# Nine groups' second MLP matmul as seven block products beside a convolution, with one weight loaded late

## The chip, the cores and the metric

The kernel runs on one core of one Trainium2 chip. The metric is device time in microseconds (us), the median of several executions. In the profile PE is TensorE's matmul, PEld its weight load, DVE is VectorE, ACT ScalarE, POOL GpSimd, SP the engine that issues most transfers; every float32 matmul leaves two PE records.

## The reference

Two blocks act on x of shape (2, 56, 56, 384), 6272 tokens of 384 channels, in float32. The first is neighbourhood attention (12 heads, 7 by 7 windows) with an MLP. The second projects to 768 channels, convolves each channel 3 by 3, smooths the result along rows and columns both ways, normalizes, projects back and ends with another MLP. Cut to what matters:

```python
# block 0
x = x + neighborhood_attention(layer_norm(x), w_qkv, rpb, w_proj)
y = layer_norm(x)
x = x + gelu(y @ w1 + b1) @ w2 + b2            # 384 -> 1536 -> 384
# block 1
p = layer_norm(x) @ w_in + b_in                # 384 -> 768
local = depthwise_conv_3x3(p, k_conv)
mixed = 0.25 * (ema_left + ema_right + ema_down + ema_up)(local) + local
x = x + layer_norm(mixed) @ w_out + b_out      # 768 -> 384
x = x + gelu(layer_norm(x) @ w1 + b1) @ w2 + b2
```

## The kernel before, in words

The attention comes first and is not touched. After it `passes` does the rest in two passes over the tokens. The first pass takes the MLP of block 0 and the projection `w_in` of block 1; the second takes `w_out` and the MLP of block 1.

**Groups.** The 49 tiles of 128 tokens are cut into `groups`: group 0 has one tile, groups 1 to 12 have four. In each group the first matmul of the MLP (`hidden`, L1206, on `columns`, L1195) goes through twelve blocks m of 128 hidden channels, three matmuls of 128x512 each. Then `project_in` runs the *previous* group's six blocks of `w_in`, whose input has been normalized meanwhile (`ahead_of`), and stores them to `p_d` in DRAM. Then the second matmul of the MLP follows.

**Two forms of the second matmul.** `tokens` (L1213) is the plain one: for each of four tiles twelve matmuls of 128x384 (`y` and `y_end` are two PSUM banks used in turn, `bank`). ScalarE has copied the residual into the bank ahead (`seeded`, L1223), and copies the result out (L1889). `tokens_by_seven` (L1669) treats the group's tokens and the hidden and output channels as 2x2 blocks and computes the product from seven block products rather than eight, 84 matmuls of 128x192. It needs sums of the hidden blocks (`sums_of_hidden`, L1644 to L1646, and `last_sum`, L1677, on GpSimd), sums of the weight blocks made once (`sums_of_w2`, L1638), and puts the products together with ScalarE copies and VectorE and GpSimd adds (L1683 to L1715). Groups 1 and 2 (`EARLY`) use the second form, as do nine groups at the end of the second pass; group 3 (`EARLY.stop`) has its first matmul by seven products and its second by `tokens`; groups 4 to 12 are plain throughout.

**The convolution beside.** From group 3 on a queue of jobs, `Beside`, is worked off on VectorE between TensorE's instructions. A `Band` is some rows of one 128-channel block of one image: eight multiply-adds (L1302) for the taps, after a first one on ScalarE (L1285) or VectorE (L1287), then a scan forth and back along the rows (L1248, L1252). A `Columns` job takes the whole plane the other way: it turns it with copies (L1348), scans it forth and back twice and adds the result to what is stored. ScalarE scales a band's result (L1317), and GpSimd issues the accumulating transfer to `mix_d` (L1321). The order on each engine is the program's, so `Beside.go` decides by bookkeeping how much of the queue stands between two steps of TensorE:

```python
def go(self, worth, own=0.0):
    self.due += self.rate * worth - own
    while self.due > 0.0:
        step = self.step()
        if step is None: self.due = 0.0
        else: self.due -= step
```

`worth` is TensorE's step (`MLP` 2.6 for a hidden block, `ROW` 7.8 for a tile of `tokens`), `rate` is 1.06, `own` what VectorE has to do besides (`STATS` 0.75 for one tile's statistics), and each step gives an estimate of its own time. Loading a job that was not loaded ahead books 8.0. `beside.later` issues transfers and scalings some steps after the work that they need. `beside.until` works the queue off up to a job; it stands before the last group, for image 0, and in the second pass before the tail, for image 1.

**Buffers.** The pool `io` has two buffers each of `mx` (a group's 768 projected channels), `xc` (a group's result x2) and hT. `w_out` is loaded at the start, and `prepare_w_out` folds the normalization into it in group 4: six narrow matmuls (L1146), a transfer of the column sums to DRAM and back (`sums_d`), and seven VectorE operations. In groups 4 to 12 the transposed inputs go through three `pt` banks (`to_channels`, L269 on TensorE and L272 on ScalarE).

Of the kernel before, what the change touches and what calls it, by code (L numbers as in the profile page):

```python
# [42 lines left out]
P = 128  # L43
# [133 lines left out]
def block_kernel(ctx: ExitStack, tc: tile.TileContext, ins: dict, out: bass.AP):  # L177
# [914 lines left out]
    def passes(xs, xn, w1, w2, between=lambda ps: None):  # L1092
# [5 lines left out]
        cctx, bctx, fctx = ExitStack(), ExitStack(), ExitStack()  # L1098
# [15 lines left out]
        w_out = wp.tile([P, NI, C], F32, name="w_out")  # L1114
# [12 lines left out]
        turns, hids = [], []  # L1127
# [11 lines left out]
        def prepare_w_out():  # L1139
# [4 lines left out]
            for c in range(NI):  # L1144
                yield
                nc.tensor.matmul(  # L1146
                    ps[:2, :], lhsT=pair[:, c, :], rhs=w_out[:, c, :],
                    start=c == 0, stop=c == NI - 1,
                )
# [8 lines left out]
            for _ in range(3):  # L1158
# [10 lines left out]
        def channels(xn, n, g, b):  # L1169
            hT = io.tile([P, NC, MT], F32, name="hT")  # L1170
            to_channels(ps_t, [xn[:, k, :] for k in range(n)], hT, NC, g, b, tag)
# [245 lines left out]
        def load_mix(g):  # L1417
            t0, n = dgroups[g]
            mx = io.tile([P, NI, MT], F32, name="mx")
# [37 lines left out]
        def measure_beside(m, g, ahead):  # L1457
# [3 lines left out]
            k = m // 2 - 1  # L1461
            if m == 4:
                add_row(ahead[1], n, "b_out")
            if m == 10:
# [6 lines left out]
        def project_out(g, mx, x, inner, then=lambda k: None):  # L1471
            n = dgroups[g][1]
            x3 = io.tile([P, NT, C], F32, name="xc")
# [15 lines left out]
        for w, name in ((w_in, "L1_conv_w_in"), (w_out, "L1_conv_w_out")):  # L1489
            nc.sync.dma_start(out=w, in_=ins[name].rearrange("(c p) n -> p c n", p=P))  # L1490
        load_row(1, "b_out")
# [6 lines left out]
        waiting = xn_w = hT_w = xn_next = cp = decay = None  # L1498
# [3 lines left out]
        def project_in(g, hT, between=lambda: None, at=1):  # L1502
            t0, n = groups[g]
            pt = io.tile([P, NI, MT], F32, name="mx")
# [125 lines left out]
        def sums_of_w2(w2, engine=nc.gpsimd):  # L1630
# [4 lines left out]
            t1, t2, t3, t4 = (tp.tile([P, q, C // 2], F32, name=f"w2_t{i}") for i in range(4))  # L1635
# [12 lines left out]
        def tokens_by_seven(low, high, s1, s2, w2, w2_sums, src, dst):  # L1648
# [10 lines left out]
            u1, u2 = (tp.tile([P, 2, hc], F32, name=x) for x in ("u1", "u2"))  # L1659
# [21 lines left out]
            def result(engine, half, c, t):  # L1681
                at = slice(2 * half, 2 * half + 2), slice(c * hc, (c + 1) * hc)
                engine.tensor_tensor(dst[:, at[0], at[1]], t, src[:, at[0], at[1]], ALU.add)  # L1683
# [13 lines left out]
            product(bank_z, 1, summed(s1), t1)  # L1697
            for p in range(2):
# [3 lines left out]
            nc.vector.tensor_tensor(u2, bank_z, u2, ALU.add)  # L1702
            product(bank_a, 1, of(high, 0), b21)
            last_sum(1)
            result(nc.gpsimd, 1, 1, u2)
            result(nc.vector, 0, 0, bank_a)
            yield
            for p in range(2):
# [3 lines left out]
            yield  # L1712
            for p in range(2):
                product(bank_z, p, of(high, 0), b22)
            nc.vector.tensor_tensor(u1, bank_z, u1, ALU.add)  # L1715
# [393 lines left out]
```

## Time and profile before

| what | value |
|---|---|
| median of 3 runs | 2569.69 us (2568.74 to 2572.11) |
| the profiled execution | 2573.64 us, of which the span of its instructions is 2571.8 |
| PE busy | 2545.4 us, 99% of the span |
| DVE busy | 1973.7 us, 77% |
| ACT busy | 1115.9 us, 43% |
| POOL busy | 560.9 us, 22% |
| granted TensorE clock | 0.996 |

A busy share is a mean over very different stages; the stage of the first pass lies between 670 and 1640 us, the convolution between 890 and 1910. Lines of groups read: source line, engine, operation, result<-inputs, shapes, count, busy time, mean duration. Lines of the timeline read: start, duration, engine, line, operation, and in brackets how long the engine had been idle and what ended that. A window's line has busy time and count for PE, PEld, DVE, ACT and POOL, then the granted clock, the share of DMA time and GB/s.

### The profile page before, as it was taken

The page shows a single profiled execution, that of the slowest core. Times are in us where ns is not written, and L with a number is a line of the kernel's source. Part 1 is how long each engine was busy: PE and PEld are TensorE (multiplying, and loading weights), DVE is VectorE, ACT ScalarE, POOL GpSimd, SP SyncE. Part 2 cuts the span into 40 slices and gives each one's busy share as a digit, 9 for nine tenths or more (in the row PEclk, how much of TensorE's full clock was granted, in tenths as well). Part 3 has the DMA queues.
Part 4 walks back from the last instruction along what each step waited for, and adds up shares of the span by engine and source line. Part 5 has one row for each costly group of instructions (what it writes and reads, how often), then busy time and mean ns, then how long its engine had stood idle before and what let it go on. Part 6 is the DMA issues. An engine that isn't in the chain of part 4 may idle for free. (4 is left out here: it accounts for less than half of the span.)

```text
span 2571.8 us, 41605 instructions
## 1 busy us (share of the span) xinstructions
PE 2545.4 (99%) x16438; PEld 1695.7 (66%) x16438; DVE 1973.7 (77%) x3785; ACT 1115.9 (43%) x2030; POOL 560.9 (22%) x610
## 2 busy tenths in 40 slices
PE   9999999999999999999999999999999999999999
PEld 5666666666688645554455555555568888888888
DVE  3888878887544299967999958988887877878861
ACT  4656555555333444344454443333762233233222
POOL 0111111111443011101110011011123333333332
PEclk9999999999999999999999999999999999999999
DMA  6432454225511256655675655777781333333210
GB/s 210 161 100 87 151 190 153 88 85 191 158 43 38 79 147 173 167 132 149 178 273 191 183 174 162 239 208 191 187 213 24 74 74 74 74 74 74 47 28 21
DMA packets 162159, 338.50 MB, mean 132 GB/s; under 512 B 12086, under 2 KB 113952, under 8 KB 159648
## 3 DMA queue, kind: packets, MB, share of 16 engines
q1 hardware_dynamic: 128064, 251.18, 29.1%
q0 software_dynamic: 28944, 57.81, 13.7%
q10 hardware_dynamic: 4944, 26.74, 3.1%
q8 instruction: 131, 2.15, 0.3%
q14 instruction: 76, 0.62, 0.1%
HBM read 171.91 MB, written 134.88 MB: 119 GB/s over the span
## 5 line engine op out<-in xcount | busy, mean ns | idle before, releaser
L1302 DVE SCALAR_TENSOR_TENSOR loc<-pt,taps,loc 128x495 f32<-128x495 f32 (+13 forms) x432 | 397.8, 921 | 25.2 <-ACT loc L1285 9.4
L1195 PE MATMUL mm<-hT,w 128*128 128x512 f32 x864 | 378.6, 593 | 0.6 <-ACT hT L272 0.6
L1195 PEld LDWEIGHTS mm<-hT,w 128*128 128x128 f32 x864 | 161.6, 190 | 193.8 <-issue 185.2
L571 ACT ACTIVATE pts<-pts 119x448 f32<-119x448 f32 (+5 forms) x396 | 210.8, 573 | 110.4 <-DVE pts L561 101.5
L561 DVE TENSOR_TENSOR pts<-sc,bias 119x448 f32<-119x448 f32 (+5 forms) x396 | 219.0, 615 | 45.7 <-PE sc L550 45.4
L1213 PE MATMUL y<-w,hid 128*128 128x384 f32 x648 | 213.6, 486 | 0.2 <-ACT y L1223 0.2
L1213 PE MATMUL y_end<-w,hid 128*128 128x384 f32 x648 | 213.4, 486 | 0.0
L404 PE MATMUL ps<-hT,wqkv 128*128 128x448 f32 x504 | 207.7, 557 | 2.1 <-ACT vs L449 1.5
L1448 DVE STREAM_TRANSPOSE turned<-mx 32x192 f32<-32x192 f32 x528 | 194.8, 369 | 6.9
L1178 DVE STREAM_TRANSPOSE hT<-xn 32x96 f32<-32x96 f32 x656 | 176.8, 270 | 26.0 <-ACT xn L255 17.6
L1206 ACT ACTIVATE hid<-mm,chan 128x512 f32<-128x512 f32 x144 | 98.5, 686 | 185.4 <-PE mm L1195 185.4
L1213 PEld LDWEIGHTS y_end<-w,hid 128*128 128x128 f32 x648 | 122.7, 190 | 84.5
L1213 PEld LDWEIGHTS y<-w,hid 128*128 128x128 f32 x648 | 122.3, 190 | 84.3 <-ACT y L1223 0.8
L1195 PE MATMUL mm<-hT,w_in 128*128 128x512 f32 x396 | 171.9, 593 | 0.6 <-DVE hid_u L1599 0.6
L404 PEld LDWEIGHTS ps<-hT,wqkv 128*128 128x128 f32 x504 | 92.5, 192 | 86.1 <-issue 76.0
L1195 PEld LDWEIGHTS mm<-hT,w_in 128*128 128x128 f32 x396 | 75.1, 190 | 94.9 <-issue 88.8
L1321 POOL DMA_DIRECT2D mix_d<-both x54 | 52.2, 966 | 350.6 <-ACT both L1317 213.4
L227 POOL TENSOR_TENSOR rs<-rs,mhalf 128x4 f32<-128x4 f32 (+4 forms) x56 | 53.8, 960 | 331.1 <-DVE rs L224 321.2
L550 PEld LDWEIGHTS sc<-qT,kT 32*100 32x100 f32 (+3 forms) x3168 | 87.8, 169 | 46.4 <-DVE sum L580 7.6
L590 PE MATMUL o<-pts,vt 100*32 100x112 f32 (+3 forms) x3168 | 116.6, 264 | 0.8 <-ACT pts L571 0.8
L620 PE MATMUL ps<-wproj,og 128*128 128x384 f32 x294 | 107.0, 504 | 2.8 <-DVE og L533 2.1
L550 PE MATMUL sc<-qT,kT 32*100 32x112 f32 (+3 forms) x3168 | 106.5, 268 | 3.1 <-DVE pts L561 3.1
(197 smaller groups left out, 4649.5 us busy)
## 6 DMA issues: line engine op xcount, KB each, us to landing
loc<-loc_d SPq DMA_DIRECT2D x24, 784.0 KB
xa<-x_d SPq DMA_DIRECT2D x24, 768.0 KB
xa<-rows POOLq DMA_DIRECT2D x24, 768.0 KB, 8.6
bias<-in_bias_t ACTq DMA_DIRECT2D x13, 1344.0 KB
p_d<-mx SPq DMA_DIRECT2D x11, 1536.0 KB
mx<-mix_d SPq DMA_DIRECT2D x11, 1536.0 KB
v_d<-vs SPq DMA_DIRECT2D x49, 192.0 KB
xr<-in_x SPq DMA_DIRECT2D x49, 192.0 KB
```

The lines of the kernel that those rows point to most:

```text
L404: nc.tensor.matmul(ps, lhsT=wqkv[:, c, m * P : (m + 1) * P], rhs=hT[:, c, half_of(n)], start=c == 0, stop=c == NC - 1,)
L550: nc.tensor.matmul(sc[i // 2][: w.keys, i % 2, q : q + TT], lhsT=kT[d, hg, w.keys_at + r * w.kc : w.keys_at + (r + w.rows) * w.kc], rhs=qT ...
L561: nc.vector.tensor_tensor(self.pts[:n, h : h + 2, lo:hi, :], sc[half][:n, :, at * TT : (at + hi - lo) * TT].rearrange("p h (c q) -> p h c ...
L571: nc.scalar.activation(t, t, AF.Exp)
L590: nc.tensor.matmul(o[i * HD : (i + 1) * HD, self.slot, :TT], lhsT=w.vt[:n, c, h * HD : (h + 1) * HD], rhs=self.pts[:n, i, c, :], start=c = ...
L620: nc.tensor.matmul(ps, lhsT=ogs[t // 7][:, c, at : at + P], rhs=wproj[:, c, :], start=c == 0, stop=c == NC - 1,)
L1178: nc.vector.transpose(hT[j : j + HD, :, k * P + i : k * P + i + HD], xn[i : i + HD, k, :].rearrange("p (c q) -> p c q", c=NC)[:, :, j : j ...
L1195: nc.tensor.matmul(ps[:, : n * P], lhsT=w[:, c, m * P : (m + 1) * P], rhs=hT[:, c, : n * P], start=c == 0, stop=c == NC - 1,)
L1206: nc.scalar.activation(t[:, : n * P], ps[:, : n * P], AF.Gelu, bias=col(b1, m))
L1213: nc.tensor.matmul(ps, lhsT=t[:, k * P : (k + 1) * P], rhs=w[:, m, :], start=m == 0 and onto is None, stop=m == len(lhs) - 1, skip_group_c ...
L1302: nc.vector.scalar_tensor_tensor(to, pt[:, lo + dy - self.top : hi + dy - self.top, xt : xt + n], self.tap(dy, dx), to, ALU.mult, ALU.add,)
L1448: nc.vector.transpose(t[j : j + HD].rearrange("p (m c) -> p m c", m=NI)[:, :, i : i + HD], mx[i : i + HD, :, k * P + j : k * P + j + HD],)
```

## The change

Groups 3 to 11, nine of them, take `tokens_by_seven` in place of `tokens`. In groups 4 to 11 the first matmul stays plain, and `sums_of_hidden` follows each pair of its blocks that belong together, at m = 7, 9 and 11. The last group, 12, keeps `tokens`.

The sums of the weights and of the hidden blocks get a pool of their own, `dp`, that lives until the last group. Room for it is made in two ways: `mx` and `xc` have one buffer until then, and `w_out` is no longer loaded at the start. At the last group `dp` is closed, a pool `late` takes its place with the second buffers and `w_out`, and `prepare_w_out` moves there, with two matmuls at each step in place of one.

Inside `tokens_by_seven` the products change order (b22 before t4), the bank `y_end` is copied out by ScalarE (`uz`) so that one of the adds moves from VectorE to GpSimd, and the intermediate results lie in x2's own memory where that is free. The products need one more PSUM bank (`wide_b`), so `pt` has two buffers, and the transposes of groups 4 to 11 use `y`, `y_end` and one `pt` bank. Cut to its core:

```diff
+        w_out = late = None
+        def wide(name, shape):
+            second[name] = late is not None and not second[name]
+            return late.tile(...) if second[name] else io.tile(shape, F32, name=name, bufs=1)
...
         def prepare_w_out():
             ps = bank()
             for c in range(NI):
-                yield
+                if c % 2 == 0:
+                    yield
...
-            for _ in range(3):
+            for _ in range(2):
                 yield
...
         def channels(xn, n, g, b):
-            to_channels(ps_t, [xn[:, k, :] for k in range(n)], hT, NC, g, b, tag)
+            to_channels(
+                ps_t, [xn[:, k, :] for k in range(n)], hT, NC, g, b, tag,
+                banks=[t() for t in turning] if turning else None,
+            )
...
         def measure_beside(m, g, ahead):
-            k = m // 2 - 1
-            if m == 4:
+            k = m // 2 - (2 if g == 0 else 1)
+            if m == 4 and g:
                 add_row(ahead[1], n, "b_out")
-            if m == 10:
+            if m == 10 and g:
                 ahead[2].close(n)
...
         def tokens_by_seven(low, high, s1, s2, w2, w2_sums, src, dst):
+            if src is dst:
+                u1, u2, uz = (tp.tile([P, 2, hc], F32, name=x) for x in ("u1", "u2", "u3"))
+            else:
+                u1, u2, uz = part(dst, 0, 1), part(dst, 1, 1), part(dst, 1, 0)
...
             product(bank_z, 1, summed(s1), t1)
+            nc.scalar.copy(uz, bank_z)
+            product(bank_a, 1, of(high, 0), b21)
+            last_sum(1)
+            yield
+            result(nc.vector, 0, 0, bank_a)
             for p in range(2):
                 product(bank_b, p, of(low, 1), t3)
             nc.scalar.copy(u2, bank_b)
             yield
-            nc.vector.tensor_tensor(u2, bank_z, u2, ALU.add)
-            product(bank_a, 1, of(high, 0), b21)
-            last_sum(1)
+            nc.gpsimd.tensor_tensor(u2, uz, u2, ALU.add)
             result(nc.gpsimd, 1, 1, u2)
-            result(nc.vector, 0, 0, bank_a)
+            for p in range(2):
+                product(bank_z, p, of(high, 0), b22)
             yield
+            nc.vector.tensor_tensor(u1, bank_z, u1, ALU.add)
+            result(nc.gpsimd, 0, 1, u1)
             for p in range(2):
                 product(bank_b, p, of(high, 1), t4)
             yield
             result(nc.vector, 1, 0, bank_b)
-            yield
-            for p in range(2):
-                product(bank_z, p, of(high, 0), b22)
-            nc.vector.tensor_tensor(u1, bank_z, u1, ALU.add)
-            result(nc.gpsimd if src is dst else nc.vector, 0, 1, u1)
...
+            seven = early or half_early or 0 < g < last
             if g == last:
                 beside.until((0, NI - 1))
+                dctx.close()
+                late = pctx.enter_context(tc.tile_pool(name="late", ...))
                 ahead = load_mix(0)
+                w_out = late.tile([P, NI, C], F32, name="w_out")
+                load_weights(w_out, "L1_conv_w_out")
+                preparing = prepare_w_out()
                 beside.rate = 0.98
+                for t in (y_end_wide, ps_y.tile([P, MT], F32, name="turn", tag="y")):
+                    primed(t)
...
                     hid.append(hidden(w1, m, hT, n, "L0_conv_b1"))
+                    if seven and m % 2 == 1 and m > NHID // 2:
+                        u = (m - NHID // 2) // 2
+                        sums_of_hidden(u, hids[-4], hids[-1], s1, s2)
...
+            elif seven:
+                for i, _ in enumerate(tokens_by_seven(low, high, s1, s2, w2, w2_sums, x, x2)):
+                    beside.go(ROW / 2, 2 * STATS + 0.5 if i == 6 else 0.5 if i in (3, 5) else 0.0)
+                    if i == 6:
+                        for k in range(2):
+                            norm.add(k, [x2[:, k, :]])
...
-            for k in range(n) if g >= EARLY.stop else ():
+            for k in range(n) if g == last else ():
                 ps = tokens(hid, w2, k, onto=seeds.pop(0))
```

## The prediction

> **What bounds the kernel now.** I read the busy line first, then the stretch of the nine changed groups, then who waits there, then the two forms of the matmul in order of time. The page:
>
> ```profile
> PE 2545.4 (99%) x16438; PEld 1695.7 (66%) x16438; DVE 1973.7 (77%) x3785; ACT 1115.9 (43%) x2030; POOL 560.9 (22%) x610
> ```
>
> TensorE is the bound. Groups 4 to 11 and then the stretch to the tail, by window (columns: PE, PEld, DVE, ACT, POOL busy):
>
> ```profile
> 912.31:1557.40 645.09, 645.09 (x1838) 330.30 (x1837) 555.18 (x636) 276.39 (x429) 85.30 (x76) 1.00 0.62 176
> 1557.40:1920.20 362.80, 360.26 (x1109) 195.40 (x1108) 317.37 (x359) 174.99 (x261) 61.14 (x54) 1.00 0.74 198
> ```
>
> PE never pauses in these eight groups (645.09 of 645.09), but VectorE, which runs the convolution beside it, has only 89.9 us to spare, 11.2 a group. Nearly all of it is one wait, for the next band's rows when the job queue has run dry:
>
> ```profile
> DVE loc L1287 <- DMA pt<-p_d: 87.4, 5, 26.1
> ```
>
> **What the change buys on PE.** One group in the old form, in order of time, then an early group that has the new form already:
>
> ```profile
> 1046.83 7.91 PE L1213 MATMUL y<-w,hid 128*128 128x384 f32 x24
> ...
> 1070.05 7.90 PE L1213 MATMUL y_end<-w,hid 128*128 128x384 f32 x24
> 1077.79 7.46 PE L1195 MATMUL mm<-hT,w 128*128 128x512 f32 x17
> ```
>
> ```profile
> 805.25 4.06 PE L1669 MATMUL y<-w,hid 128*128 128x192 f32 x24
> ...
> 828.65 4.06 PE L1669 MATMUL y_end<-w,hid 128*128 128x192 f32 x24
> 832.55 1.03 PE L1580 MATMUL ua<-hT,w 128*128 128x256 f32 x4
> ```
>
> Old: 1077.79 - 1046.83 = 30.96 us for 96 records of 128x384. New: 832.55 - 805.25 = 27.30 us for 168 records of 128x192. Saved 3.66 us a group, times 9: **-32.9 us**.
>
> [...] where the two meet, at the tail's weight sums:
>
> ```profile
> 1911.95 1.35 DVE L1638 TENSOR_TENSOR w_t<-w 128x1152 f32<-128x1152 f32 x1
> 1913.34 2.02 DVE L1638 TENSOR_TENSOR w_t<-w,w_t 128x1152 f32<-128x1152 f32 x1
> 1915.28 1.87 DVE L1638 TENSOR_TENSOR w_t<-w 128x1152 f32<-128x1152 f32 x1
> 1917.07 1.88 DVE L1638 TENSOR_TENSOR w_t<-w,w_t 128x1152 f32<-128x1152 f32 x1
> ```
>
> ```profile
> 1912.82 1.31 POOL L1561 TENSOR_TENSOR xsums<-hT 128x256 f32<-128x256 f32 x1
> 1914.21 1.73 POOL L1561 TENSOR_TENSOR xsums<-xsums,hT 128x256 f32<-128x256 f32 x1
> 1915.90 1.84 POOL L1561 TENSOR_TENSOR xsums<-hT 128x256 f32<-128x256 f32 x1
> ```
>
> One 1152-wide VectorE sum takes 1.35 us, but 1.87 to 2.02 with a 256-wide GpSimd sum between each two; the GpSimd sum, 0.72 us elsewhere, takes 1.73 to 1.84. They take turns: a 256-wide GpSimd sum costs VectorE about 0.57 us. In the attention part a 384-wide one costs 0.77:
>
> ```profile
> 127.66 1.39 DVE L580 TENSOR_TENSOR sum<-pts 100x448 f32<-100x448 f32 x1 [0.31 <-ACT pts L571]
> 129.09 0.62 DVE L582 TENSOR_TENSOR sum<-sum,pts 100x448 f32<-100x448 f32 x1
> ```
>
> ```profile
> 127.58 0.99 POOL L614 TENSOR_TENSOR xr<-xr,shift 128x384 f32<-128x384 f32 x1
> ```
>
> A 512-wide one (1.27 us alone, L1644) is not seen against such a neighbour. Continuing 0.57, 0.77 gives 1.0; [...] I take 1.0. [...]
>
> **Part by part.**
>
> *GpSimd sums beside the convolution.* A group gains nine 512-wide sums (`sums_of_hidden`), six 256-wide (`last_sum`) and three 384-wide adds: 9 x 1.0 + 6 x 0.57 + 3 x 0.78 = 14.7 us [...] 13.7 us. VectorE itself gains three adds from PSUM at 0.557: 1.67 us. [...]
>
> *VectorE's budget in groups 4 to 11.* Busy 555.2 now. The seven operations of `prepare_w_out` leave: -3.5. `Beside` books 1.06 x (12 x 2.6 + 6 x 2.6 + 4 x 7.8) - 6.0 = 76.7 us of convolution a full group, and then 1.06 x (46.8 + 7 x 3.9) - 7.5 = 71.0; carried through with its dry spells (a dry start books 8.0 without work: three before, two after) the eight groups do some 3 us less. Need after: 555.2 - 3.5 - 3 + 8 x 1.67 + 8 x 13.7 = 672. What PE leaves: 645.1 - 8 x 3.66 - 5.6 (w_out's six matmuls leave) + 4 (below) = 614. **VectorE falls 58 us behind.** It may lag: a job's ScalarE multiply is issued eight steps later and its accumulate eleven, ScalarE and GpSimd take their queues in order, and three mm banks cover 7.7 us of hidden matmuls; ScalarE's copies between the seven products have about 2 us. I put that at 11 us (8 to 16, from steps of 0.77 us). The rest, **+47 us**, PE waits: first at the copies of bank_a and bank_b behind a late `both` multiply, and at the sums `last_sum` behind a late accumulate.
>
> *Transposes into y, y_end and one pt bank.* bank_a is needed at once after them. ScalarE's first hT copy (0.78 us) starts at 1046.3 to 1046.8 in the group shown, so ends 0.3 to 0.8 us after PE's 1046.83: 0.5 x 9 = **+4.5** (2 to 8).
>
> *Single mx and xc buffers.* p_d's store has some 60 us until the buffer is written again, x2's store some 30: 0. If SP were that late, PE would wait; I see lags of a few us there. *ScalarE*: seeds and copies go (8 x 0.48 us), four copies come: 0, idle cover. *Early and tail groups*: same matmuls, one VectorE add becomes a ScalarE copy and a GpSimd add, VectorE does transposes there[...]: 0 (-2 to 2).
>
> *Last group.* Two priming matmuls wait for VectorE's add on y_end: its lag less 3.9 us, counted above. w_out (1152 KB) now queues on SP behind mx (1536) and xa (768), and all wait for the last product's weights. At the 364 GB/s that one window reached it lands after 10 us, at 240 after 15; its first matmul, at m = 7, comes after 19: 0 to 8, I take 2. Leaving SP's queue at the start gains nothing, PE waits there for nothing of SP. The sums' round trip over SP (`sums_d`, two reads) has two steps, 5.2 us, instead of three until VectorE adds it; if it is late VectorE waits in order, some us of its 45 idle ones: 0. The accumulating `add_row` on GpSimd goes behind project_in; it lands in 8.6 us by the page and has four token tiles, 31 us: 0. Before the tail, three steps of the last column job remain where one did: two scans, 6.8 us, ahead of the weight sums, with about 2 us of slack to PE's next need of VectorE: 5. Together **+7** (0 to 20). The rest of that stretch has 45 us of idle VectorE for 8 us more convolution, w_out's 3.5 and the lag: 0.
>
> Sum: -32.9 + 47 + 4.5 + 7 = **+25.6 us**. The profiled execution took 2573.64 (span 2571.8), 3.95 over the median of 2569.69. 2573.64 + 25.6 - 3.95 = **2595 us**.
>
> **Rivals.**
> 1. [...] The taps' longest, 1.327 us for about 1045 elements, shows no lengthening beside today's small GpSimd powers, and 87 us of dry waiting is there to be filled. With no stall: -32.9 + 4.5 + 7 = -21.4, **2548**. It decides at a loss of 10.5 us a group (562 + 8x - 614 - 11 = 21.4); I price 13.7. Against it: the alternation above.
> 2. *GpSimd's queue is the tighter one (much slower).* The second `last_sum` has 3.75 us until its product; where column jobs run, each of its three sums may wait for a scan of 3.4: 12.4 - 3.75 = 8.6 us, in four groups +35: **2630**.
> 3. Both sides cancel: **2570**.
>
> **How the numbers follow.** My case 0.55 (own range 2575 to 2625), rival 2 0.14, rival 1 0.23, rival 3 0.08. The range 2545 to 2640 leaves out the ends of the rivals. About 0.2%, 5 us, is what a measurement here can tell from no change: faster 0.23, same 0.08, slower 0.69.
>
> **What would show it.** Right: the seven products at 27.3 us plus gaps, a group period above 79.9 us instead of 77, PE waiting for ScalarE, GpSimd and VectorE some 50 us in groups 4 to 11, VectorE busy near 2090 us, its taps longer on average than 921 ns. Wrong: taps at 921 and a period of 77 (rival 1); or gaps before y_end's last product while VectorE is idle (rival 2).

## The result, and the profile after

The changed kernel takes 2650.84 us (median of 4 runs, 2649.88 to 2655.11) against 2570.9 us for the kernel before, run beside it: a ratio of 1.0315, 95% interval 1.0297 to 1.0333. It is slower by 80 us. The prediction was 2595 us, range 2545 to 2640: the sign is right, the size is not, and the result lies outside the range. The profiled execution took 2655.11 us (span 2653.3), 4.3 over the median, as the one before lay 3.95 over its own median of 2569.69; the two profiles can be subtracted.

The page of the kernel after, its busy line (engine, busy us, share of the span, instructions):

```profile
PE 2543.1 (96%) x17085; PEld 1790.6 (67%) x17087; DVE 2078.8 (78%) x3798; ACT 1104.4 (42%) x2006; POOL 853.0 (32%) x785
```

TensorE's share has gone from 99% to 96%, and it is busy for as long as before although nine groups have less to multiply. VectorE gained 105 us, GpSimd 292. The windows of the same two stretches as before, groups 4 to 11 and then up to the tail (columns: PE, PEld, DVE, ACT, POOL busy, granted clock, DMA share, GB/s):

```profile
910.10:1624.92 714.82, 638.55 (x2404) 415.00 (x2403) 660.05 (x653) 259.19 (x396) 341.43 (x221) 0.95 0.56 159
1624.92:1997.76 372.84, 366.77 (x1120) 196.60 (x1119) 323.75 (x371) 176.82 (x262) 57.29 (x52) 0.99 0.73 198
```

The eight groups take 714.8 us instead of 645.1, the rest up to the tail 372.8 instead of 362.8. Set against the start of the span: group 4 begins 2.2 us earlier, the last group 67.5 later, the tail 77.6 later, the end comes 81.5 later. So 69.7 of the 81.5 us are in groups 4 to 11. There the clock is 0.95, and PE stands still for 76.3 of 714.8 us, while VectorE too is idle for 54.8. VectorE's one large wait of before, for the next band's rows, is still there, smaller. In groups 4 to 11 before, and then after (us in total, times, longest):

```profile
DVE loc L1287 <- DMA pt<-p_d: 61.3, 4, 25.5
```

```profile
DVE loc L1300 <- DMA pt<-p_d: 24.0, 2, 12.0
```

The products themselves are as short as predicted where nothing waits: 27.40 us in group 3, from 882.70 to 910.10. Group 9 after, in order of time (start, us, operation, count, idle before):

```profile
1410.78 4.17 PE L1691 MATMUL y<-w,hid 128*128 128x192 f32 x24 [1.06 <-ACT hT L272]
...
1436.15 4.06 PE L1691 MATMUL yb<-w_t,hid 128*128 128x192 f32 x24
...
1440.05 2.31 PE L1208 MATMUL mm<-hT,w 128*128 128x512 f32 x5
```

From 1410.78 to 1440.05 are 29.27 us, with a pause of 1.60 inside: 27.67 without it. What PE waits for in groups 4 to 11, after (us in total, times, longest):

```profile
PE y L1691 <- ACT hT L272: 27.2, 6, 10.8
PE mm L1208 <- ACT hT L272: 13.0, 2, 6.9
PE mm L1208 <- ACT hid L1219: 11.0, 4, 3.5
PE turn L269 <- ACT xn L255: 9.0, 2, 8.7
PE y_end L1240 <- DVE xc L1733: 8.5, 1, 8.5
PE mm L1208 <- ACT mx L1522: 5.5, 2, 4.2
```

All but one of the waits name ScalarE, and none GpSimd. ScalarE is busy for 36% of the stretch, so it is late, not full. And the turns of VectorE and GpSimd that the prediction had priced are there to be read. VectorE and GpSimd after, in order of time, while group 4's sums run beside the taps (the convolution's multiply-adds):

```profile
940.89 11.09 DVE L1315 SCALAR_TENSOR_TENSOR loc<-pt,taps,loc 128x990 f32<-128x990 f32 x5
```

```profile
941.93 2.21 POOL L1661 TENSOR_TENSOR hid<-hid 128x512 f32<-128x512 f32 x1
944.12 2.27 POOL L1659 TENSOR_TENSOR s<-hid 128x512 f32<-128x512 f32 x1
946.47 2.16 POOL L1660 TENSOR_TENSOR s<-s,hid 128x512 f32<-128x512 f32 x1
948.58 2.27 POOL L1661 TENSOR_TENSOR hid<-hid 128x512 f32<-128x512 f32 x1
```

Five taps take 11.09 us, 2.22 each, and the four sums start 2.1 to 2.4 us apart: one of each by turns. In e13 (below) four such taps, with GpSimd doing nothing beside them, take 5.15 us, 1.29 each. By the difference a 512-wide sum costs VectorE 0.93 us; the prediction had 1.0.

### The profile page after: what moved, and what is told of

Read it like the earlier page. It is cut to its first block, busy times and chain, and to the rows that moved or that the text cites. A ratio compares the mean times of both kernels' runs of the same rounds, so it can differ in the third digit from the quotient of the medians.

```text
span 2653.3 us, 43196 instructions
## 1 busy us (share of the span) xinstructions
PE 2543.1 (96%) x17085; PEld 1790.6 (67%) x17087; DVE 2078.8 (78%) x3798; ACT 1104.4 (42%) x2006; POOL 853.0 (32%) x785
## 5 line engine op out<-in xcount | busy, mean ns | idle before, releaser
L1315 DVE SCALAR_TENSOR_TENSOR loc<-pt,taps,loc 128x495 f32<-128x495 f32 (+13 forms) x432 | 458.5, 1061 | 22.1 <-ACT loc L1298 9.6
L1208 PE MATMUL mm<-hT,w 128*128 128x512 f32 x864 | 387.2, 604 | 12.5 <-ACT hid L1219 11.7
L1699 POOL TENSOR_TENSOR hid<-hid,s 128x256 f32<-128x256 f32 x120 | 123.8, 1056 | 245.6 <-PE y L1691 245.6
L1691 PE MATMUL y<-w,hid 128*128 128x192 f32 x960 | 172.8, 335 | 27.6 <-ACT hT L272 27.2
L1208 PE MATMUL mm<-hT,w_in 128*128 128x512 f32 x396 | 180.7, 616 | 19.1 <-ACT hT L272 13.0
L1691 PEld LDWEIGHTS y<-w,hid 128*128 128x128 f32 x960 | 163.4, 196 | 32.4 <-ACT hT L272 29.7
L1691 PE MATMUL yb<-w_t,hid 128*128 128x192 f32 x960 | 162.7, 326 | 1.6 <-ACT xc L1716 1.6
L1208 PEld LDWEIGHTS mm<-hT,w_in 128*128 128x128 f32 x396 | 77.6, 198 | 119.7 <-issue 91.6
L1691 PEld LDWEIGHTS yb<-w_t,hid 128*128 128x128 f32 x960 | 157.0, 190 | 1.9 <-ACT xc L1716 1.9
L516 POOL COPY totals<-turned 128x12 f32<-128x12 f32 x56 | 20.5, 366 | 391.7 <-DVE turned L511 391.7
L1659 POOL TENSOR_TENSOR s<-hid 128x512 f32<-128x512 f32 x60 | 90.6, 1510 | 154.3 <-ACT hid L1602 127.3
```

What stands on the lines that cost most here:

```text
L1208: nc.tensor.matmul(ps[:, : n * P], lhsT=w[:, c, m * P : (m + 1) * P], rhs=hT[:, c, : n * P], start=c == 0, stop=c == NC - 1,)
L1315: nc.vector.scalar_tensor_tensor(to, pt[:, lo + dy - self.top : hi + dy - self.top, xt : xt + n], self.tap(dy, dx), to, ALU.mult, ALU.add,)
L1659: nc.gpsimd.tensor_tensor(s1[:, at], low[:, :, b], high[:, :, b], ALU.add)
L1691: nc.tensor.matmul(bank[:, p, :], lhsT=lhs(c, p), rhs=w[:, c, :], start=start and c == 0, stop=c == q - 1, skip_group_check=True,)
L1699: nc.gpsimd.tensor_tensor(to, to, s2[:, 2 * u : 2 * u + 2, p * P : (p + 1) * P], ALU.subtract)
```

## The experiments

All times are medians; the kernel before was timed beside each and lay at 2569 to 2571 us. Two questions ran through them: is it VectorE's time that is lost, and how does it turn into pauses of TensorE? "Groups 4 to 11" is the stretch of the windows above: 645.1 us before, 714.8 after; some 612 is what TensorE needs there after the change (its busy time in e6 below). The attention, which no version changes, varies from one profile to the next (its last matmul starts at 673.3 us in the kernel before and at 663.7 in e11), so stretches of profiles are compared below rather than whole spans.

### First round: what is lost

**e1_no_sums.** Groups 4 to 11 without the fifteen block sums on GpSimd (`sums` is true in group 3 alone).

```diff
-                    if seven and m % 2 == 1 and m > NHID // 2:
-                        u = (m - NHID // 2) // 2
-                        sums_of_hidden(u, hids[-4], hids[-1], s1, s2)
...
             def last_sum(p):
-                for u in range(q // 2):
+                for u in range(q // 2 if sums else 0):
```

> Leaves out the 15 GpSimd block sums (sums_of_hidden, last_sum) in groups 4 to 11; the three adds per group stay. Theory A ([...] VectorE falls behind, its lag reaches TensorE through ScalarE's and GpSimd's queues): VectorE busy in groups 4 to 11 falls from 660 to about 575 us, the pauses of TensorE there nearly vanish, about 2550 to 2560 us in all against 2651. Theory B (the new order of the banks makes TensorE wait for ScalarE's hT copies whatever VectorE does): pauses before the seven products stay, some 2610 us.

Measured: 2576.13 us, ratio 1.0027 (1.0016 to 1.0039). So the sums cost 75 of the 80 us. Its windows line for groups 4 to 11:

```profile
901.30:1541.50 640.20, 617.93 (x2405) 407.01 (x2404) 572.73 (x653) 261.49 (x396) 133.96 (x101) 0.99 0.62 178
```

The same 653 VectorE instructions take 572.7 us instead of 660.1: the sums cost VectorE 87.3 us, **10.9 a group**. But this is not the 2550 to 2560 of theory A: there are pauses left, 13.9 us of them at the first product, which waits for hT.

**e2_banks.** hT's three transposes in the two pt banks and y_end, so that the first product's bank y is free of them.

```diff
-                turning[:] = [
-                    lambda: ps_y.tile([P, MT], F32, name="turn", tag="y"), lambda: y_end_wide,
-                    lambda: ps_t.tile([P, MT], F32, name="turn", tag="pt"),
-                ]
+                turning[:] = [lambda: ps_t.tile([P, MT], F32, name="turn", tag="pt")] * 2
+                turning.append(lambda: y_end_wide)
```

> The changed kernel, but the transposes of groups 4 to 11 go to two pt banks and y_end, so that bank_a (y) is free at once and y_end only 3.9 us later. Theory A: VectorE's load stays 660 us and it is the budget that decides, so the wait moves on to the next tight place; 5 to 25 us gained, 2625 to 2645. Theory B: the 56 us of waiting for hT before products and blocks go, about 2595.

Measured: 2647.99 us, ratio 1.0303 (1.0276 to 1.033), 3 us less than after. The two intervals overlap, so this is no clear gain, and it is short of the 5 to 25 us that theory A gave. What PE waits for in groups 4 to 11 of e2:

```profile
PE y_end L1691 <- ACT hT L272: 15.4, 2, 8.4
PE mm L1208 <- ACT hT L272: 15.0, 2, 8.6
PE mm L1208 <- ACT hid L1219: 13.4, 7, 4.0
```

The wait for y has gone and come back at the next places, as theory A said. Here the bank is only the place where VectorE's shortage shows.

**e3_vector_sums.** The block sums and result adds of groups 4 to 11 on VectorE itself (with them group 3's `last_sum` and adds).

```diff
-            nc.gpsimd.tensor_tensor(s1[:, at], low[:, :, b], high[:, :, b], ALU.add)
+            engine.tensor_tensor(s1[:, at], low[:, :, b], high[:, :, b], ALU.add)
...
-                        sums_of_hidden(u, hids[-4], hids[-1], s1, s2)
+                        sums_of_hidden(u, hids[-4], hids[-1], s1, s2, nc.vector)
...
```

> All sums and adds of groups 4 to 11 on VectorE in place of GpSimd (18 operations a group). Theory A: VectorE pays its own time for them, about 9.4 us a group (0.65, 0.36 and 0.47 us each), [...] GpSimd's queue is free of them: VectorE busy about 640 us in groups 4 to 11 and 25 to 45 us gained, about 2610. [...]

Measured: 2625.16 us, ratio 1.0211 (1.0185 to 1.0237): 26 us less, at the small end of theory A's 25 to 45. VectorE is busy for 634.1 us in groups 4 to 11, where it was 660.05 with GpSimd's sums. The sums as groups of VectorE's instructions in e3 (count, then busy us and mean ns of one):

```profile
L1699 DVE TENSOR_TENSOR hid<-hid,s 128x256 f32<-128x256 f32 x54 | 20.7, 420 | 53.5 <-PE y L1691 53.5
L1660 DVE TENSOR_TENSOR s<-s,hid 128x512 f32<-128x512 f32 x24 | 16.6, 692 | 0.8
```

A group's sums take VectorE 9 x 0.69 + 6 x 0.42 = 8.7 us when it makes them, and cost it 10.9 (e1) when GpSimd makes them. Had they cost it nothing there, VectorE would only have gained work, and the kernel would have become slower, not faster.

**e4_pauses.** The kernel *before*, with twenty extra copies on ScalarE ahead of the second matmul, so that PE stops once in each of groups 4 to 11 and does the same work.

```diff
+            for _ in range(20 if EARLY.stop < g < last else 0):
+                nc.scalar.copy(seeds[0], x[:, 0, :])
             for k in range(n) if g >= EARLY.stop else ():
```

> The kernel before, with the first bank of the second matmul copied 20 times over by ScalarE ahead of groups 4 to 11, which makes TensorE pause about 8.4 us in each of the eight and changes nothing else. If a pause costs its own length alone: 2570 + 67 = 2637 us. If TensorE's clock is granted lower for a while after a pause, as the changed kernel's 0.95 in groups 4 to 11 suggests: 2 to 3 us more for each, about 2657, with a clock below 0.98 in those groups.

Measured: 2686.3 us, ratio 1.0447 (1.0419 to 1.0474). Two of its eight pauses in order of time; this product took 7.91 us before:

```profile
974.58 9.49 PE L1213 MATMUL y<-w,hid 128*128 128x384 f32 x24 [11.63 <-ACT y L1885]
...
1162.58 11.05 PE L1213 MATMUL y<-w,hid 128*128 128x384 f32 x24 [11.62 <-ACT y L1885]
```

The pauses are 95.9 us together, 12 each where 8.4 were expected, and PE is busy for 665.2 us in groups 4 to 11 instead of 645.1: 20.1 us, **2.5 us for each pause**, on top of it. The granted clock from 900 to 1600 us is 0.94, where it is 1.00 in groups 4 to 11 of the kernel before.

### Second round: how the loss becomes a pause

**e5_no_multiply.** Groups 4 to 11 without ScalarE's multiply of `both`, the instruction with which ScalarE waits for VectorE's scans.

```diff
-                beside.later(lambda: nc.scalar.mul(flat(both), flat(both), share), 8)
+                beside.later(lambda: beside.rate == 1.06 or nc.scalar.mul(flat(both), flat(both), share), 8)
```

> The changed kernel with ScalarE's multiply of `both` by share left out in groups 4 to 11 (the accumulate then adds the unscaled sum; that part of the computation is changed). The sums and the convolution on VectorE stay. Theory A (VectorE's lateness reaches TensorE through ScalarE's queue, which it takes in order: a multiply that waits for a late scan holds the hT, hid and mx copies behind it): most of the 75 us of pauses go, and with them most of the 24 us that the lower clock took: about 2585 us, 2570 to 2605. Theory B (VectorE simply has too little time, 660 us of work in the 638 us that TensorE leaves, and what it is late by ends up as a pause somewhere): the waits move to the sums of the hidden tiles, the priming and the adds on VectorE, and the time stays at 2630 to 2650 us.

Measured: 2638.32 us, ratio 1.0262 (1.0243 to 1.0281). My theory A, that ScalarE's order is the road on which nearly all of it travels, falls: 12.5 us, not 65; the time is in theory B's range. Its windows for groups 5, 6, 7 and 11:

```profile
982.40:1077.70 95.30, 83.50 (x302) 53.59 (x301) 91.56 (x106) 27.88 (x44) 36.43 (x31) 0.91 0.58 149
1077.70:1164.00 86.30, 78.87 (x302) 51.09 (x301) 74.39 (x99) 25.56 (x41) 33.97 (x30) 0.96 0.52 126
1164.00:1248.00 84.00, 78.94 (x303) 51.46 (x302) 71.68 (x92) 25.81 (x41) 33.38 (x29) 0.98 0.52 133
...
1503.60:1606.20 102.60, 81.62 (x304) 53.15 (x303) 100.82 (x85) 27.77 (x42) 47.43 (x28) 0.90 0.58 171
```

Groups 6 and 7 went from 100.0 and 91.5 us after to 86.3 and 84.0; groups 5 and 11 from 93.5 and 95.7 to 95.3 and 102.6. In the latter VectorE is busy for 96% and 98%: there it is itself the limit, with the multiply or without. In 6 and 7 it was order.

**e6_none_apart.** e1, with e2's banks, and with a dry job queue no longer issuing all that stands in `late` at once.

```diff
-        due = [x for x in self.late if x[0] < 0 or got is None]
+        due = [x for x in self.late if x[0] < 0]
```

> The kernel without the block sums of groups 4 to 11 (e1_no_sums, 2576 us), with the three transposes of hT in the two pt banks and y_end instead of y, y_end and pt, and with a dry job queue no longer issuing all that is due later at once. The sums are left out as there, so the products of these groups use sums of an earlier group. Theory A (what is left of the loss in e1 is the hT copies that stand behind a `both` multiply with product 1 waiting for bank y): the 12.7 us or more of pauses go, eight groups take 617 to 622 us instead of 640, and the time is about 2553 us, 2547 to 2562. Theory B (it comes from elsewhere, say from the clock or from the convolution's rows): 2570 to 2576 us.

Measured: 2561.62 us, ratio 0.9968 (0.9957 to 0.9979), theory A at the upper end of its range: groups 4 to 11 take 621.1 us, of which PE is busy for 612.1 at a clock of 1.00. So order it was that cost e1 its last 15 us. It is what the new products give if the sums were free: 8 us, not 33. From the last group's start to the end it takes 1033.6 us, as e1 does, where the kernel before takes 1014.4.

**e7_rate.** 15% less convolution issued beside groups 4 to 11.

```diff
                 decay = flat(decay)
+                beside.rate = 0.9
```

> The changed kernel with Beside's rate at 0.9 instead of 1.06 in groups 4 to 11: 15% less convolution is issued beside each group, as if the time that GpSimd's sums take from VectorE were booked. Theory A (the pauses come from VectorE's being issued more than it can do, so that it is 20 us behind TensorE's place in the program): the pauses in groups 4 to 11 fall from 75 to under 35 us, the clock stays near 1.0, and what was not issued, some 40 us, is done ahead of the last group, in part beside it: about 2625 us, 2605 to 2640. Theory B (the amount doesn't matter, each `both` multiply waits for its scan all the same): 2645 to 2655 us.

Measured: 2731.43 us, ratio 1.0636 (1.0616 to 1.0656), outside both expectations. Its windows, groups 4 to 11 and then the hidden part of the last group, and PE's largest wait:

```profile
901.30:1555.10 653.80, 619.77 (x2404) 407.40 (x2403) 601.57 (x614) 256.39 (x389) 329.46 (x219) 0.98 0.56 157
1555.10:1723.20 168.10, 41.42 (x110) 18.25 (x109) 138.71 (x114) 31.20 (x42) 8.29 (x11) 0.62 0.56 162
```

```profile
PE mm L1208 <- ACT hid L1219: 102.3, 1, 102.3
```

The pauses in groups 4 to 11 fell to 34.0 us as theory A said. What it had wrong is the debt: the convolution that wasn't issued, which must be done before the last group can begin, kept VectorE busy for 138.7 us there, and PE stood still for 102.3 us at a stretch. VectorE's work was moved in time here, but found no empty place.

**e8_vector_apart.** All sums computed, on VectorE: e3 with two edits more, e2's to `turning` and e6's to `due`.

> All of it computed: the changed kernel with the block sums and adds of groups 4 to 11 on VectorE (e3_vector_sums, 2625 us), the hT transposes in the two pt banks and y_end, and a dry job queue no longer issuing all at once. Theory A (hT copies behind a late multiply cost as much here as in e1, and the last_sum on VectorE is the next wait): 10 to 15 us less than e3, 2610 to 2617 us. Theory B (as in e2, the wait moves on to the next bank): 2622 to 2628 us.

Measured: 2606.75 us, ratio 1.0139 (1.012 to 1.0158), 18 less than e3 and 44 less than after: more than theory A's 10 to 15. The largest wait that is left is for VectorE's `last_sum` (26.7 us at y_end's last product).

### Third round: order alone, and fewer groups

**e9_order.** The changed kernel with GpSimd's sums, the same two edits, and the priming of y and y_end in the last group moved from its start into the loop over m.

```diff
-                for t in (y_end_wide, ps_y.tile([P, MT], F32, name="turn", tag="y")):
-                    primed(t)
...
+                    if m == 5 and g and not seven:
+                        for t in (y_end_wide, ps_y.tile([P, MT], F32, name="turn", tag="y")):
+                            primed(t)
```

> The changed kernel, GpSimd's sums and all, with its order alone put right: hT's transposes in the two pt banks and y_end, a dry job queue no longer issuing at once all that is due later, and the last group's two priming matmuls at m = 5 instead of ahead of m = 0. Theory A (two losses: in six groups VectorE is full and they last as long as its work, 523 us by the windows; in groups 6 and 7 it runs dry, and there the hT copies wait behind a multiply issued right behind its scan, 9.4 and 10.8 us of pause, and VectorE then waits 12 us for rows that the paused TensorE delivers late): groups 6 and 7 together go from 191 to 160 to 170 us, the full ones stay: about 2622 us, 2612 to 2635. Theory B (VectorE's shortage sets the total, and whatever wait is taken away comes back elsewhere, as in e2): 2640 to 2650 us.

Measured: 2631.56 us, ratio 1.0239 (1.0223 to 1.0254): 19 us less, within theory A's range, at its slow end. Groups 6 and 7 take 175 us instead of 191, not 160 to 170.

**e12_vector_order.** e8 with that priming.

> All sums and adds of groups 4 to 11 on VectorE, the hT banks and the dry queue as in e8_vector_apart (2607 us), and the last group's priming at m = 5. Both theories: the 5.7 us that the priming waited go, 2598 to 2604 us. A shortage that reappears elsewhere (theory B) would leave 2605 to 2610.

Measured: 2600.01 us, ratio 1.0119 (1.0105 to 1.0134), 6.7 less than e8, as expected. It is the best version with seven products in all nine groups, and still 1.2% slower than before.

**e10_three, e11_three_vector.** Seven products only in groups 3, 6, 7 and 11, with e9's order; the sums are GpSimd's in e10 and VectorE's in e11. The other groups take the old second matmul, and the bookkeeping follows. Which groups those are is read from windows of the kernel before, one for each group; here groups 5, 6, 7, 10 and 11:

```profile
997.90:1077.80 79.90, 79.90 (x230) 41.25 (x229) 74.74 (x112) 33.73 (x55) 12.56 (x13) 1.00 0.64 160
1077.80:1157.70 79.90, 79.90 (x229) 41.27 (x228) 56.70 (x86) 31.02 (x51) 10.40 (x11) 1.00 0.52 131
1157.70:1237.70 80.00, 80.00 (x230) 41.33 (x229) 61.56 (x92) 31.36 (x51) 10.83 (x11) 1.00 0.59 150
...
1397.50:1477.50 80.00, 80.00 (x230) 41.32 (x229) 77.86 (x77) 34.61 (x50) 9.36 (x9) 1.00 0.59 167
1477.50:1557.40 79.90, 79.90 (x230) 41.25 (x229) 53.19 (x54) 29.31 (x46) 11.24 (x7) 1.00 0.57 172
```

Of VectorE's 89.9 us to spare, 68.3 lie in groups 6, 7 and 11; the other five have 2 to 5 us each.

```diff
-            seven = early or half_early or 0 < g < last
+            seven = early or half_early or g in (6, 7, 11)
```

> Seven products only in group 3 and in groups 6, 7 and 11, where VectorE had 18 to 27 us to spare before the change; groups 4, 5, 8, 9 and 10, where it had 2 to 5 us, keep the old second matmul on seeded banks. GpSimd makes the sums; order as in e9_order. Theory A (the loss comes from groups whose VectorE was full): no group is longer than TensorE's work; 4 x 3.66 = 14.6 us less, 6 us more in the tail (its pauses there after the change), so 2570 - 14.6 + 6 = about 2561 us, 2555 to 2568. Theory B (beside any convolution at all the sums cost more than 3.66 us a group, by order and clock): 2572 to 2590 us.

> As e10_three, with the sums and adds of these three groups on VectorE instead of GpSimd. Theory A: VectorE's spare time in these groups covers 9 to 10 us of sums [...] so within 4 us of e10_three: 2557 to 2567 us. Theory B ([...] GpSimd's queue also holds the accumulates): 5 to 15 us less than e10_three.

Measured: e10 2585.03 us, ratio 1.0064 (1.0051 to 1.0077), and e11 2574.13 us, ratio 1.0015 (1.0007 to 1.0023). In both, groups 6 and 11 add onto bank yb without its being primed after a group of the old form, so a part of one sum is lost there. Theory A falls in both. e10 lies where theory B put it, and e11 is 11 us below it, as B said: GpSimd's sums cost more than VectorE's even in groups with room. e10's PE pauses for 14.9 us from group 3 to the last one, 6.9 of them ahead of the projection in group 6, straight behind the full group 5. e11's pauses for 4.2, in a profile that is the fastest of its sixteen executions (2565.94 us), so more than that may be usual.

### Fourth round: memsets for sums, and the version computed in full

**e13_memsets.** Each block sum on GpSimd is replaced by three memsets of the same destination: GpSimd is kept busy and writes the same tiles, but reads none.

```diff
-            nc.gpsimd.tensor_tensor(s1[:, at], low[:, :, b], high[:, :, b], ALU.add)
+            for _ in range(3):
+                nc.gpsimd.memset(s1[:, at], 0.0)
...
```

> The changed kernel with each of the fifteen block sums of a group (groups 4 to 11) replaced on GpSimd by three memsets of the same destination: by the memset of 1568 elements (1.4 us) some 1.4 us in place of a 512-wide sum's 1.27, and 0.7 in place of a 256-wide one's 0.72, so GpSimd is as busy as a sum alone would keep it, but reads nothing. The products get zeros for the sums; that part of the computation is changed. Theory A (VectorE loses its time [...]): VectorE needs 570 to 585 us in groups 4 to 11 as without the sums, and the time is 2575 to 2590 us. Theory B (GpSimd's occupied queue is what delays the accumulates, the normalisation and so VectorE and TensorE): VectorE may need less, but the pauses stay, 2625 to 2650 us.

Measured: 2574.38 us, ratio 1.0014 (1.0002 to 1.0026), 0.6 us under theory A's range. Theory A, that VectorE loses its time to the sums themselves and not to GpSimd's being busy, holds. Groups 4 to 11 of e13, then the taps' group of e13 and of the kernel after (busy us, mean ns of one):

```profile
905.10:1544.40 639.30, 617.88 (x2404) 406.98 (x2403) 573.07 (x653) 261.84 (x396) 287.91 (x461) 0.99 0.61 178
```

```profile
L1315 DVE SCALAR_TENSOR_TENSOR loc<-pt,taps,loc 128x495 f32<-128x495 f32 (+13 forms) x432 | 406.0, 940 | 26.2 <-ACT loc L1298 13.7
```

```profile
L1315 DVE SCALAR_TENSOR_TENSOR loc<-pt,taps,loc 128x495 f32<-128x495 f32 (+13 forms) x432 | 458.5, 1061 | 22.1 <-ACT loc L1298 9.6
```

GpSimd is busy for 287.9 us beside the convolution, twice as long as in e1, and VectorE's 653 instructions take 573.1 us as in e1 (572.7; e1's taps have the same mean, 940 ns). The same can be read from single stretches. Eight taps of one band in e13 beside the memsets of group 4, a row of these memsets, and the next band's eight taps, when GpSimd has none left:

```profile
928.57 10.55 DVE L1315 SCALAR_TENSOR_TENSOR loc<-pt,taps,loc 128x990 f32<-128x990 f32 x8
```

```profile
931.68 3.31 POOL L1658 MEMSET s<- 128x512 f32 x6
```

```profile
944.08 10.54 DVE L1315 SCALAR_TENSOR_TENSOR loc<-pt,taps,loc 128x990 f32<-128x990 f32 x8
```

Here GpSimd's memsets, which only write, cost VectorE nothing; its sums, which read as well, cost it 10.9 us a group.

**e14_three_fixed, e15_two_fixed.** e11 with yb primed where it has to be, and with hT's transposes in the last group beginning with the bank that the tail wants first; e15 leaves group 6 in the old form.

```diff
+                    if m == 5 and seven and g - 1 not in (3, 6, 7, 11):
+                        primed(wide_b)
```

> All of it computed: seven products in groups 3, 6, 7 and 11, their sums on VectorE, as in e11_three_vector (2574 us), with the bank yb primed by one more matmul where a group of the old form came before, and in the last group hT's transposes start with the bank that the tail needs first. Theory A (four times 3.66 us less on TensorE, 6 us of pauses more near the tail, of which 1.5 to 2.8 go by the order of the banks, 4 us of pause in group 6): 2563 to 2571 us, within 0.3% of the kernel before. Theory B (the sums cost more than the products save wherever they are put): over 2575 us.

> As e14_three_fixed, with seven products in groups 3, 7 and 11 only; group 6, which took over VectorE's lag from the full group 5 and paused 4 us in e11, keeps the old form. Theory A: 3.66 us less gained and 4 us less paused, equal to e14 within 3 us, 2563 to 2571 us. Theory B: 3 to 8 us less than e14.

Measured: e14 2573.98 us, ratio 1.0017 (1.001 to 1.0024); e15 2573.99 us, ratio 1.0024 (1.0014 to 1.0035). They are equal, as expected, but 3 us beyond the range. In e14's profile groups 4 to 11 take 638.9 us against 645.1 before; with w_out's matmuls gone and three times 3.66 us saved they would take 628.5. Of the 10 us between, 7.7 are in group 6 (a pause of 4.3 us, a clock of 0.96), and the five groups of the old form are each 0.4 to 0.7 us longer than before. From the last group's start to the end e14 takes 1029.7 us, 15.3 more than before, of which w_out's matmuls, which moved there, are 5.6. None of the versions that compute everything beats the kernel before.

## Why the prediction was right or wrong

| Term | Predicted | Measured |
|---|---|---|
| seven products in place of four | 27.30 us a group | 27.40 in group 3 |
| VectorE's work for groups 4 to 11 | 672 us, 661 of it within them | 660.05 within them |
| of it the fifteen sums, a group | 11.5 us | 10.9 (e1) |
| groups 4 to 11: PE's pauses | 47 us and 4 at the transposes | 76.3 |
| groups 4 to 11: PE busy | 610 us | 638.55 (612.1 in e6, at a clock of 1.00) |
| groups 4 to 11 in all | 661 us | 714.8 |
| last group and tail, with w_out's matmuls | +12.6 | +14.0 |

**Right: what was lost, and where.** TensorE's gain, the cost of the sums and VectorE's work came near what was forecast. The last group and the tail came within 1.4 us in the sum, but that is in part luck: 10.0 us lie ahead of the tail, where 12.6 were forecast, and 4 in the tail, where nothing was. That the convolution would take turns with GpSimd's sums as the weight sums do was an estimate before the run; group 4's taps show it (2.22 us each beside the sums, 1.29 alone), and e13 shows that GpSimd's being busy is not enough for it: taps at 940 ns on average in the run with memsets, 1061 in the one with sums. The step from 14.7 to 13.7 us a group took 7% of VectorE's time there to be free of the turns; that was an estimate of mine, and no run here shows which instructions are free.

**Wrong: the step "VectorE falls 58 us behind. It may lag ... I put that at 11 us. The rest, +47 us, PE waits".** It pools the eight groups, as though VectorE, once it is the tighter engine, were never idle. By that sum VectorE works for 661 us of this stretch without a break (672 less the 11 of lag). It did work for 660.05, and the 54.8 us in which it was idle are the whole miss. The work is not VectorE's to do at any time: the rows of a band exist only when TensorE has delivered them. A full group had some 76 us of work before, the change adds 13.5 ((660.05 - 555.18 + 3.5) / 8), and TensorE leaves 76.2 to do it in: it is some 13 us short, and the debt goes on into the next groups. Before the change groups 6, 7 and 11 had 68 of the 90 us to spare. Windows of these three after:

```profile
1081.65:1181.64 99.99, 81.81 (x302) 53.81 (x301) 84.13 (x108) 29.51 (x49) 36.63 (x30) 0.90 0.47 118
1181.64:1273.10 91.46, 79.35 (x302) 52.84 (x301) 72.61 (x92) 29.14 (x47) 37.16 (x29) 0.93 0.47 120
...
1529.19:1624.92 95.73, 81.22 (x303) 52.89 (x303) 94.09 (x80) 29.22 (x44) 46.85 (x27) 0.94 0.59 174
```

Group 11 did take over what the groups before it had left: VectorE is busy for 94.1 us there instead of 53.2. But in groups 6 and 7, behind the full groups 4 and 5, VectorE stands idle for 15.9 and 18.9 us, more than half of the 54.8, although it comes there late.

How that happens can be read from group 7. ScalarE, then VectorE, then PE, in order of time:

```profile
1240.61 0.67 ACT L1330 ACTIVATE both<-both 128x560 f32<-128x560 f32 x1 [8.22 <-issue]
1241.19 1.25 ACT L1522 ACTIVATE mx<-mm,chan 128x512 f32<-128x512 f32 x2
1242.33 0.78 ACT L272 ACTIVATE hT<-turn,chan 128x512 f32<-128x512 f32 x1
```

```profile
1239.20 1.32 DVE L1265 TENSOR_TENSOR_SCAN both<-decay,both 128x560 f32<-128x560 f32 x1
1252.53 1.02 DVE L1300 TENSOR_SCALAR loc<-pt,taps 128x504 f32<-128x504 f32 x1 [12.00 <-DMA pt<-p_d]
```

```profile
1243.15 6.71 PE L1691 MATMUL y<-w,hid 128*128 128x192 f32 x24 [10.84 <-ACT hT L272]
```

The job queue runs dry in the program, so `step` issues all of `late`, and the multiply stands right behind its scan, with mx and hT behind it in ScalarE's queue. VectorE reaches that scan late, at 1239.2. ScalarE waits 8.2 us (its line names no releaser, but the multiply starts 0.09 us after that scan's end at 1240.52), PE 10.8 us for hT. The evictions of mx (ScalarE's copies out of PSUM) stand behind the same multiply; they are the next band's rows, which go out to p_d and come back. SP, the engine that issues these transfers, right after (SPq is its queue):

```profile
1242.46 1.05 SPq L1529 DMA_DIRECT2D p_d<-mx  x2
1249.51 0.96 SPq L1283 DMA_DIRECT2D pt<-p_d  x2
```

So VectorE in its turn waits 12.0 us. Both engines lose time to one debt. The prediction named the place ("the copies of bank_a and bank_b behind a late `both` multiply" stand a few instructions further on in the same queue), but not that the time of both would be lost. Putting the order right brings 19 us (e9), leaving out the multiply 12.5 (e5). The greater part is left then; e5's groups 5 and 11, in which VectorE is busy nearly throughout, point to VectorE's lack of time itself. I had argued for the order as the main road after e1 and was wrong in that.

**Missing: the clock.** The sum had a pause cost its length, and no term for the time after it. After the 10.84 us above the first 24 matmuls take 6.71 us; after 1.06 us, in group 9, they take 4.17. e6 runs as many matmuls in groups 4 to 11 at a clock of 1.00 in 612.1 us, the changed kernel at 0.95 in 638.55: 26 us. Counted on TensorE, the miss in groups 4 to 11 is 25 us of pauses and 28 of busy time, nearly all of it clock. It can be read in windows around that pause: the granted clock is 1.00 from 1230 to 1232 us, 0.50 from 1236 to 1243, still 0.50 in the first 4.9 us of the product (1243.1 to 1248.0), and 1.00 from 1248.5 on. One matmul behind the pause takes 0.687 us at most instead of 0.326. In the first 4.2 us of group 9's product, behind its 1.06 us, the clock is 1.00. How long a pause has to be to lower it, no run here shows. e4 gives the price: 2.5 us for each pause of about 12.

**The transposes** at 0.5 us a group hold only while ScalarE is in time. With VectorE late, 27.2 us of waiting stood there, and e2 shows that it would have stood elsewhere.

**The rivals.** Rival 1, by which the turns cost VectorE hardly anything and which decides at 10.5 us a group, was refuted in its premise: the sums alone cost 10.9. Even e6, without them, does not reach its 2548. Its 87 us of dry waiting were misread, too: the line of 87.4 us covers 880 to 1560 us, and 26.1 of it lie in group 3; in groups 4 to 11 it is 61.3 of VectorE's 89.9 us. (Its tap of 1.327 us has 1064 elements, not 1045.) Rival 2, GpSimd's queue as the tighter one, is not seen: none of PE's waits above names GpSimd. e13 tests it only in part, since memsets fill the queue but took only 0.55 us each beside the taps, where a sum took over 2.

**Left open.** e9 leaves groups 6 and 7 at 175 us where TensorE needs 152; I have not divided the rest into debt and order. Nor is it known which part of the change lengthens the stretch from the last group's start to the end: 1014.4 us before, 1028.4 in the changed kernel, 1029.7 in e14 and 1033.6 in e1 and e6 (one profile each), although these differ in VectorE's load. w_out's moved matmuls are 5.6 us of it; the rest, 8 to 14 us, is more than half of what the products save in e14.

## What to carry to other kernels

Before giving GpSimd work to spare VectorE, measure what it costs VectorE beside the work that runs there; here VectorE made the same sums in 8.7 us a group (e3) and lost 10.9 to having them made (e1). Count an engine's spare time in the stretch where it is needed, not over the stage: 68 of 90 us lay in three groups of eight, and the five full ones were each some 13 us short. And price a pause of TensorE above its length when it is long: each of some 12 us cost 2.5 more here (e4).

## What the runs showed of the hardware that I had not expected

- GpSimd's memsets beside the convolution cost VectorE nothing (573.1 us against 572.7 without them), at 287.9 us of GpSimd's time; its sums, 341.4 us of GpSimd's time with the queue's own work, cost 87 us.
- The turns are not quite the sum of both: a tap alone took 1.29 us and a 512-wide sum alone 1.27 us, but a tap and a sum by turns 2.22 us, not 2.56.
- A pause of 11.6 us lengthened the product behind it by 1.6 us in one group and 3.1 in another of the same kernel (e4: 9.49 and 11.05 us instead of 7.91), so the price of one pause was not fixed here.
